# A graph kernel's second pass: gathers tied one by one to TensorE's products, small products placed behind dense ones, and the first block turned in two halves

## The chip, the cores and the metric

The kernel runs on one core of one Trainium2 chip, in one launch. The metric is the device time of that launch in microseconds; less is better. Beside times, a profile of one execution is read: per engine (TensorE = PE, VectorE = DVE, ScalarE = ACT, GpSimd = POOL, SyncE = SP) what ran when, what each waited for, and what the DMA queues moved.

## The reference

Two layers of a graph network over 3327 nodes with 512 features, padded to 3328 = 26 blocks of 128. `adj` is a 3327 x 3327 matrix with few non-zero entries, most of them in the first rows and columns ("hubs"), since the chance of an edge falls with both node numbers.

```python
# layer 0
h = relu(layernorm(x))
g = relu(adj @ (h @ W1) + b1)            # W1: 512 x 128
x = x + adj @ (g @ W2) + b2              # W2: 128 x 512
# layer 1
h = relu(layernorm(x))
attn_a = sigmoid(concat([adj @ h, h]) @ Wa.T + ba)      # one number a node
attn_b = sigmoid(concat([adj @ h, h]) @ Wb.T + bb)
hw = h @ W_sa
scores = (hw @ a_left)[:, None] + (hw @ a_right)[None, :]
e = where(adj != 0, exp(-leaky_relu(scores, 0.01)), 0)
x_a = (e / (e.sum(1) + 1e-5)) @ hw
x_b = adj @ (h @ W_gcnb) + b_gcnb
x = x + sigmoid(attn_a * x_a + attn_b * x_b)
```

## The kernel before, in words

Everything is float32. Columns of `adj` transposed are taken in chunks of 512 (the last of 256); `adj` is used in four ways.

*First pass* (line 549 on): for each chunk, `acc_u` adds 26 dense products of `u = h @ W1` with a 128 x 512 tile of `adj` (L568); the result becomes `g` and is also stored to DRAM. DVE looks through the same tiles (L572), and `make_lists` (L433) makes from that, for every block, lists of the rows with entries: step by step (`yield`), one step for each dense product. POOL gathers by these lists the 128 x 32 pieces of `adj` that have entries (`gather_adj`, `gather_behind`), each tied by `pace` to a dense product.

*Second pass* (L818): `adj @ g`. The last two chunks of nodes (blocks 18 to 25) are "listed": their sums are made from gathered rows of `g` (`gather_g`, 48 gathers) by small products (`list_sums`, L784). The five other chunks (`dense_chunks`, the fifth of 256 columns) are dense: 26 products each (L825), every tile of `adj` loaded by SP. Between the dense products the loop calls generators that record other work:

- `make_h1` (L639): for each block of a finished chunk load `x` (`xb`), add `b2` (L650), the product `px` with `W2` (L663), add it (L666), store, layer-normalise and relu into a row tile (`ln_relu`, L244), two scores (L623), the block's own logits (L630), and store the row to `h_dram` (L637). At a chunk's end the scores of its blocks are transposed by TensorE (`pl`, L687).
- `hubs` (`add_hubs`, L704) and `make_e_hub` (L729): block 0 (the hubs) is dense in layer 1. For every block, `acc_hub[0]` adds a product with `a_hub`, `acc_hub[1]` one with `e_hub`, the exponentials made by DVE and ACT (L709). Row tiles stand in a ring of 12 (`NR`), `e_hub` in a ring of 8 (`EH`).

`SUMS` names the dense products behind which `list_sums` goes a step; the other calls follow from the product's number `n`. `queued(x)` records what follows behind instruction `x` in the order of its engine; beyond that a scheduler decides the order on each engine from the recorded dependencies. After the loop the rest of the hub products is recorded (L871).

*Sparse stage* (L903 on): for blocks 25 down to 1, POOL gathers rows of `h_dram` (194 gathers, which wait until all rows are stored), `attend` (L917) makes their exponentials on DVE and ACT, `sums` (L968) adds small products into `acc` (L981), `turn` (L988) transposes the two sums (`ptt`, L995), `weigh` (L1026) multiplies them with `W_gcnb` (`p_b`, L1035) and `W_sa` (`p_a`, L1042), and `finish` (L875) ends the block and stores it. Adjacency pieces that are not yet gathered follow two a block (`fetch_ae`). The first block to be weighed is block 0, from `acc_hub`: both its halves are turned behind block 25's sums (L1079 to L1082).

Of the kernel before, what the change touches and what calls it, by code (L numbers as in the profile page):

```python
# [50 lines left out]
def kernel(  # L51
# [207 lines left out]
    with (  # L259
# [173 lines left out]
        def make_lists(nth, most):  # L433
# [56 lines left out]
            for batch in batches:  # L490
# [7 lines left out]
                for i, q in batch:  # L498
                    r, k = rooms[i], col[i, q]
                    for h in range(2):  # L500
                        b = NQ * i + 2 * h + q - g0
                        nc.vector.tensor_scalar(
                            at[:, k : k + r, h, :],
                            place_row[:, : r * HALF].rearrange("p (k m) -> p k m", m=HALF),
                            offset[:, b : b + 1], None, op0=ALU.is_ge,
                        )
                    yield
                pl = bank(psB, f"p_list_{f0}")
                plv = pl[:, : m * NT].rearrange("p (c j) -> p c j", j=NT)
# [129 lines left out]
        def make_h1(c, sT, last):  # L639
# [16 lines left out]
            for b, i in enumerate(blocks):  # L656
# [21 lines left out]
                if not extra[i] and i not in LATE:  # L678
                    own_logits(
                        i, made_row(i),  # L680
                        l0w.tile([P, D], BF16, tag="junk", name=f"junk_{i}", bufs=1),
                    )
                yield
            n = w // P
            pl = bank(psB, f"pl_{c0}")
            for b, i in enumerate(blocks):
# [11 lines left out]
            rows_made.update(blocks)  # L698
            yield

        rows_made, unstored = set(), []
        last_row = [None, None, None]

        def add_hubs():  # L704

            def add(k, i, s, n):
                nc.tensor.matmul(  # L709
                    acc_hub[k], s, made_row(i)[:, :D], start=(n == 0), stop=(n == NB - 1)  # L710
                )

            for n, i in enumerate(made_order):
                while i not in rows_made:
                    yield
                add(0, i, a_hub[:, i, :], n)
                if i not in e_hub:
                    make_e_hub()
                yield
                if n:  # L720
                    before_i = made_order[n - 1]
                    add(1, before_i, e_hub[before_i], n - 1)
                    e_added.add(before_i)
                    yield
            add(1, made_order[-1], e_hub[made_order[-1]], NB - 1)
# [25 lines left out]

        g_slots, g_rows, g_taken, g_tile = slots(), {}, [], [None]

        def gather_g(n):
            for f in g_slots:
                k = len(g_taken) % NU
                if not k:
                    g_tile[0] = l0w.tile([P, D], F32, tag="h", name=f"g_row_{f}", bufs=GR // NU)
                t = g_tile[0][:, k * HID : (k + 1) * HID]
                g_taken.append(f)  # L760
                gather(t, g_dram[:, :], row_h[:, f : f + 1], NP - 1)
                g_rows[f] = t
                n -= 1
                if not n:
                    break

        def list_sums():

            for c0, w in listed_chunks:
                acc = bank(psB, f"acc_s_{c0}")  # L770
                for b, i in enumerate(range(c0 // P, (c0 + w) // P)):
                    r = rooms[i] + extra[i]
                    assert fetched[i] == 2 * rooms[i]
                    for k0, k1 in segments(i):
                        for kk in range(k0, k1):
                            for q in range(2):
# [4 lines left out]
                                for h in range(2):  # L781
# [6 lines left out]
                                    )  # L788
                    gather_g(2 * rooms[i])
                    yield  # L790
                s = l0w.tile([P, CW], F32, tag="x", name=f"s_{c0}", bufs=5)
                nc.scalar.copy(s[:, :w], acc[:, :w])
                pt = bank(psB, f"pt_s_{c0}")
                for b in range(w // P):
# [18 lines left out]
        QUIET = 6  # L813
        SUMS = {1: (14, 16, 18, 20, 24), 2: (16, 18, 20, 22, 25)}
        summing = list_sums()
        gather_g(GR)
        order = [i for c0, w in back for i in range(c0 // P, (c0 + w) // P)]
        for c, (c0, w) in enumerate(dense_chunks):  # L818
# [3 lines left out]
            for n, j in enumerate(order):  # L822
# [5 lines left out]
                if c == 0 and n >= 2:  # L828
                    next(lists, None)
                if n in SUMS.get(c, ()):  # L830
                    next(summing)
                elif c and n % 4:
                    gather_behind(added)
                if n % 2 or (c in (2, 3) and n % 4 == 2):
                    with queued(last_e[0] if last and n < 8 else None):
                        next_late()
                if last and n >= NB - QUIET:
                    continue
                if c > 1 and n % 3 == 2:
                    next(hubs)  # L840
                elif c > 1 and (n > 8 if last else n % 3 == 1):
                    with queued(last_row[0] if last else None):
                        make_e_hub()
            if c == 0:
# [11 lines left out]
        while late:  # L856
            next_late()
        for i in unstored:
            store_row(i)
# [11 lines left out]
    with queued(*last_row):  # L871
        for _ in hubs:
            pass

# [28 lines left out]
    with tc.tile_pool(name="spw", bufs=2) as spw:  # L903
# [83 lines left out]

        def turn(i, ty, both_engines):  # L988


            tyT = spw.tile([P, KD, 2, P], F32, tag="tyT", name=f"tyT_{i}")
            for h in range(2):
                pt = bank(psA, f"ptt_{i}_{h}")
# [31 lines left out]

        def weigh(i, tyT, es, cuts=(0, D), sums_first=False):  # L1026

# [5 lines left out]
            for n in (1, 0):  # L1033
                for k in range(KD):
                    nc.tensor.matmul(  # L1035
                        p_b[n][:, :WH], tyT[:, k, 0, :], W_g_sb[:, k, n * WH : (n + 1) * WH],
                        start=(k == 0), stop=(k == KD - 1),
                    )
            p_a = bank(psB, f"p_a_{i}")
            for c0, c1 in zip(cuts, cuts[1:]):  # L1040
                for k in range(KD):
                    last = nc.tensor.matmul(  # L1042
                        p_a[:, c0:c1], tyT[:, k, 1, :], W_sa_sb[:, k, c0:c1],
                        start=(k == 0), stop=(k == KD - 1),
                    )
            return (
# [17 lines left out]

        with queued(last_e[1]):
            for seg in segments(NB - 1):
                made = attend(NB - 1, seg)

        def own_of(i, inst):
# [3 lines left out]

        own_of(LATE[0], made[0])
        fetch_ae(AE_PER)
        for seg in segments(NB - 1):
            added = sums(NB - 1, seg)
        combined.append(added)
        with queued(made[1]):  # L1079
            ty, _ = copy_out(0, acc_hub)  # L1080
        with queued(added):
            tyT, added, copied = turn(0, ty, False)  # L1082
        own_of(LATE[1], copied)
        weighing = 0, tyT, es_hub
        ty, last = copy_out(NB - 1, taken[NB - 1]["acc"])
        turning = NB - 1, ty, taken[NB - 1]["es"]
        held = [copied, last]
        for i in range(NB - 2, 1, -1):
            with queued(*held):
                for seg in segments(i):  # L1090
                    made = attend(i, seg)
            if i == NB - 2:
                own_of(LATE[2], made[0])
            fetch_ae(AE_PER)
# [227 lines left out]
```

## Time and profile before

| | |
|---|---|
| median of 9 runs | 733.88 us (732.98 to 738.29) |
| the profiled execution's own time | 735.72 us |
| its span, first to last instruction | 734.0 us |
| granted TensorE clock, mean | 0.986 |
| dense products of the second pass, `acc_g` (L825) | 112.1 us busy, 260 passes |
| products of the sparse stage, `p_b` (L1035) and `p_a` (L1042) | 97.1 and 93.5 us busy |
| hub products, `acc_hub` (L709) | 104 passes, 281.4 to 413.9 us |
| gathers on POOL: `ae`, `hr`, `rows`, `g_row` | 194, 120, 74 and 48 |
| DMA in the second pass's middle (242 to 322 us) | 320 GB/s, mean busy share 0.96 |

A float32 product appears in the trace as two passes. Their recorded durations overlap, since they are pipelined, so the cost of one is read from start to start: two passes of 512 columns take 0.858 us. A line of the timeline gives the start, the time covered, the engine, the line of the kernel, the operation and, in brackets, how long the engine was idle before and what ended that. By stages of the span: the first pass runs to about 218 us, the second to about 392, the rest of the hub products to 414, and the sparse stage from there to the end.

### The profile page before, as it was taken

The page shows a single profiled execution, that of the slowest core. Times are in us where ns is not written, and L with a number is a line of the kernel's source. Part 1 is how long each engine was busy: PE and PEld are TensorE (multiplying, and loading weights), DVE is VectorE, ACT ScalarE, POOL GpSimd, SP SyncE. Part 2 cuts the span into 40 slices and gives each one's busy share as a digit, 9 for nine tenths or more (in the row PEclk, how much of TensorE's full clock was granted, in tenths as well). Part 3 has the DMA queues.
Part 4 walks back from the last instruction along what each step waited for, and adds up shares of the span by engine and source line. Part 5 has one row for each costly group of instructions (what it writes and reads, how often), then busy time and mean ns, then how long its engine had stood idle before and what let it go on. Part 6 is the DMA issues. An engine that isn't in the chain of part 4 may idle for free.

```text
span 734.0 us, 11907 instructions
## 1 busy us (share of the span) xinstructions
PE 704.7 (96%) x3595; PEld 394.9 (54%) x3595; DVE 507.0 (69%) x1625; ACT 193.8 (26%) x402; POOL 466.8 (64%) x490
## 2 busy tenths in 40 slices
PE   9999988999999999898999899999999999999995
PEld 7775433444464444343455366566565666565653
DVE  7778978999985657988887255556566465746452
ACT  6872000000000124335544112223122222212211
POOL 2400476777765777777666777777777777777400
PEclk9999999999999999999999999999999999999999
DMA  8778899999979999989984856667788888787600
GB/s 274 247 273 265 281 328 289 299 309 290 308 206 309 332 327 360 310 282 321 299 280 136 262 154 201 210 198 219 228 260 275 261 238 275 231 251 235 197 29 33
DMA packets 104889, 185.08 MB, mean 252 GB/s; under 512 B 18401, under 2 KB 35441, under 8 KB 104818
## 3 DMA queue, kind: packets, MB, share of 16 engines
q1 hardware_dynamic: 66544, 113.43, 46.4%
q0 software_dynamic: 23264, 57.64, 27.4%
q10 hardware_dynamic: 15010, 13.18, 5.5%
q8 instruction: 30, 0.49, 0.3%
q14 instruction: 41, 0.34, 0.1%
HBM read 162.29 MB, written 22.26 MB: 251 GB/s over the span
## 4 chain that ended last, share of the span: by engine, by line
PE 75%; DMA 12%; DVE 9%; issue 2%; ACT 1%; POOL 0%; SPq 0%; POOLq 0%; DVEq 0%; ACTq 0%
PE acc_u L568 13%; PE acc L981 13%; PE p_b L1035 13%; PE p_a L1042 12%; PE acc_g L825 8%; DMA a<-in_adjT_dram 6%; DMA xb<-in_x_dram 4%; PE pu L333 3%; PE ptt L995 3%; DVE most L572 2%; PE acc_hub L709 2%; PE pt L325 1%; PE px L663 1%; DVE junk L623 1%; DMA x<-xb 1%
## 5 line engine op out<-in xcount | busy, mean ns | idle before, releaser
L166 POOL DMA_INDIRECT ae<-in_adjT_dram,row_a x194 | 203.4, 1049 | 126.4 <-DVE past L519 54.3
L568 PE MATMUL acc_u<-a,rows 128*128 128x512 f32 (+1 forms) x364 | 160.6, 578 | 5.2 <-DMA a<-in_adjT_dram 5.2
L166 POOL DMA_INDIRECT hr<-h_rows,row_h x120 | 122.6, 1022 | 36.9 <-issue 22.9
L572 DVE TENSOR_REDUCE most<-a 128x16 f32<-128x512 f32 (+1 forms) x182 | 112.0, 639 | 12.8 <-DMA a<-in_adjT_dram 12.5
L825 PE MATMUL acc_g<-a,g 128*128 128x512 f32 (+1 forms) x260 | 112.1, 565 | 0.7 <-DMA a<-in_adjT_dram 0.7
L568 PEld LDWEIGHTS acc_u<-a,rows 128*128 128x128 f32 x364 | 66.1, 194 | 63.9 <-issue 48.8
L1035 PE MATMUL p_b<-W_g_sb,tyT 128*128 128x257 f32 x416 | 97.1, 385 | 0.8 <-ACT tyT L1008 0.5
L166 POOL DMA_INDIRECT rows<-h_rows,row_h x74 | 77.7, 1050 | 25.3 <-issue 11.9
L1042 PE MATMUL p_a<-W_sa_sb,tyT 128*128 128x512 f32 (+2 forms) x216 | 93.5, 576 | 0.0
L1035 PEld LDWEIGHTS p_b<-W_g_sb,tyT 128*128 128x128 f32 x416 | 76.5, 189 | 30.9 <-DVE ae L249 5.7
L1010 DVE COPY tyT<-ptt 128x512 f32<-128x512 f32 x51 | 34.9, 687 | 71.1 <-PE ptt L995 71.1
L825 PEld LDWEIGHTS acc_g<-a,g 128*128 128x128 f32 x260 | 48.6, 194 | 49.9 <-issue 41.8
L166 POOL DMA_INDIRECT g_row<-g_rows,row_h x48 | 51.5, 1072 | 19.5 <-issue 13.7
L1042 PEld LDWEIGHTS p_a<-W_sa_sb,tyT 128*128 128x128 f32 x216 | 40.9, 189 | 37.8 <-issue 35.9
L981 PE MATMUL acc<-hr,ae 64*64 64x512 f32 x480 | 57.7, 598 | 0.0
L884 ACT ACTIVATE f<-f 128x2 f32<-128x2 f32 x26 | 5.3, 203 | 164.2 <-DVE f L883 141.1
L343 ACT ACTIVATE gT<-acc_u,b_col 128x512 f32<-128x512 f32 (+1 forms) x7 | 4.6, 657 | 150.5 <-DMA a<-in_adjT_dram 93.7
L623 DVE SCALAR_TENSOR_TENSOR junk<-rows,w_rows 128x512 bf16<-128x512 f32 x52 | 35.7, 687 | 4.6 <-ACT rows L244 3.6
L981 PE MATMUL acc<-rows,ae 64*64 64x512 f32 x296 | 36.3, 609 | 1.9 <-DVE ae L251 1.9
L981 PEld LDWEIGHTS acc<-hr,ae 64*64 64x64 f32 x480 | 26.0, 135 | 20.0 <-issue 19.7
L995 PEld LDWEIGHTS ptt<-ident,ty 128*128 128x128 f32 x208 | 24.2, 141 | 14.7 <-issue 13.9
L666 DVE TENSOR_TENSOR xb<-px,xb 128x512 f32<-128x512 f32 x26 | 17.2, 683 | 21.4 <-PE px L663 21.4
(159 smaller groups left out, 938.1 us busy)
## 6 DMA issues: line engine op xcount, KB each, us to landing
a<-in_adjT_dram SPq DMA_DIRECT2D x286, 256.0 KB
h_rows<-rows SPq DMA_DIRECT2D x26, 260.0 KB
x<-in_x_dram SPq DMA_DIRECT2D x26, 256.0 KB
xb<-in_x_dram SPq DMA_DIRECT2D x26, 256.0 KB
x<-xb ACTq DMA_DIRECT2D x26, 256.0 KB
x1b<-x SPq DMA_DIRECT2D x26, 256.0 KB
out_dram<-va SPq DMA_DIRECT2D x25, 256.0 KB
ae<-in_adjT_dram,row_a POOLq DMA_INDIRECT x194
```

What stands on the lines that cost most here:

```text
L166: return nc.gpsimd.indirect_dma_start(out=dst, out_offset=None, in_=table, in_offset=bass.IndirectOffsetOnAxis(ap=rows, axis=0), bounds_ch ...
L333: nc.tensor.matmul(pu[:, :HID], hT[:, k, :], W1_sb[:, k, :], start=(k == 0), stop=(k == KD - 1))
L568: added = nc.tensor.matmul(acc[:, :w], u[j], a[:, :w], start=(j == 0), stop=(j == NB - 1))
L572: nc.vector.tensor_reduce(most[:, : w // GW, j], a[:, :w].rearrange("p (b i) -> p b i", i=GW), axis=AX.X, op=ALU.max, apply_absolute_value ...
L623: return nc.vector.scalar_tensor_tensor(junk, h, 1.0, w_rows[:, s, :], op0=ALU.mult, op1=ALU.mult, accum_out=into)
L666: nc.vector.tensor_tensor(x1, px, x1, ALU.add)
L825: added = nc.tensor.matmul(acc[:, :w], g[j], a[:, n % per, :], start=(n == 0), stop=(n == NB - 1))
L981: added = nc.tensor.matmul(taken[i]["acc"][h][q * HALF : (q + 1) * HALF, :], both[half_p, q * n + k, :], taken[i][k0][k][half_p, q, :D], s ...
L995: moved = nc.tensor.transpose(pt[:, k * P : (k + 1) * P], ty[h][:, k * P : (k + 1) * P], ident)
L1010: last = nc.vector.tensor_copy(dst, src)
L1035: nc.tensor.matmul(p_b[n][:, :WH], tyT[:, k, 0, :], W_g_sb[:, k, n * WH : (n + 1) * WH], start=(k == 0), stop=(k == KD - 1),)
L1042: last = nc.tensor.matmul(p_a[:, c0:c1], tyT[:, k, 1, :], W_sa_sb[:, k, c0:c1], start=(k == 0), stop=(k == KD - 1),)
```

## The change

1. In `make_lists` a step is added between the making of a batch's flags (`at`) and its products.
2. The transposes of a chunk's scores leave `make_h1` for a function `turn_logits`; it is called behind the second block of the next chunk's `make_h1` (for the last chunk at once).
3. `gather_g` fetches one row set, and `gather_one` is called from the loop for one gather at a time: of `g` while slots are free, else of `adj`. Each is tied by `pace` to the dense product it stands behind and recorded behind the gather before it. A running sum `owed` (0.93 for a dense product, more where px or hub products stand) sets how often: one each 1.4. Before, 24 gathers of `g` were issued at once and the others after each block's list sums, and `gather_behind` stood behind three products of four.
4. All that the loop records behind a dense product (list sums, px, hub products, exponentials) is placed behind that product in TensorE's order (`queued(added)`). px begins at the third product of a chunk. `SUMS` is changed, and the copy and transposes of the list sums are two steps.
5. The rest of the hub products is recorded by `rest_of_hubs`: first pairs, then all of `acc_hub[0]`, then `acc_hub[1]` but for three, then block 0's first half is turned, then the last three.
6. Block 0's `p_b` comes ahead of block 25's sums, its second half is turned there, and blocks 25 and 24 are summed and block 25 turned before block 0's `p_a`.

```diff
@@ make_lists
                     yield
+                yield
                 pl = bank(psB, f"p_list_{f0}")
@@ make_h1
+                if b == 1 and unturned:
+                    unturned.pop()()
                 yield
+            unturned.append(lambda: turn_logits(c0, w))
+            if last:
+                unturned.pop()()
+            yield
+
+        def turn_logits(c0, w):
             n = w // P
+            blocks = range(c0 // P, (c0 + w) // P)
...
+        added_hubs = [0, 0]
+        def add_hub(k, i, s, n):
+            added_hubs[k] += 1
+            return nc.tensor.matmul(
+                acc_hub[k], s, made_row(i)[:, :D], start=(n == 0), stop=(n == NB - 1)
+            )
+        def rest_of_hubs(k, until):
+            last = None
+            for n in range(added_hubs[k], until):
+                i = made_order[n]
+                while k and i not in e_hub:
+                    make_e_hub()
+                with queued(last):
+                    last = add_hub(k, i, e_hub[i] if k else a_hub[:, i, :], n)
+                if k:
+                    e_added.add(i)
+            return last
...
+        def gather_g():
+            n = len(g_taken)
+            f = g_slots[n]
+            if n % NU == 0:
+                g_tile[0] = l0w.tile([P, D], F32, tag="h", name=f"g_row_{f}", bufs=GR // NU)
+            g_rows[f] = g_tile[0][:, n % NU * HID : (n % NU + 1) * HID]
+            g_taken.append(f)
+            return gather(g_rows[f], g_dram[:, :], row_h[:, f : f + 1], NP - 1)
+        def gather_one(matmul):
+            n = len(g_taken)
+            with queued(last_g[0]):
+                if n < len(g_slots) and n // NU * NU < len(g_summed) // NU * NU + GR:
+                    made = gather_g()
+                else:
+                    made = next(columns, None)
+            if made is not None:
+                pace(made, matmul)
+                last_g[0] = made
@@ list_sums
-                    gather_g(2 * rooms[i])
+                    g_summed.extend(2 * rooms[i] * [i])
                     yield
                 s = l0w.tile([P, CW], F32, tag="x", name=f"s_{c0}", bufs=5)
                 nc.scalar.copy(s[:, :w], acc[:, :w])
+                yield
@@ the loop
-        SUMS = {1: (14, 16, 18, 20, 24), 2: (16, 18, 20, 22, 25)}
+        STEP, SPACE, owed = 0.93, 1.4, 0.0
+        SUMS = {1: (14, 16, 18, 20, 21, 25), 2: (17, 20, 22, 25), 3: (0, 4)}
-        gather_g(GR)
...
-                if n in SUMS.get(c, ()):
-                    next(summing)
-                elif c and n % 4:
-                    gather_behind(added)
-                if n % 2 or (c in (2, 3) and n % 4 == 2):
-                    with queued(last_e[0] if last and n < 8 else None):
-                        next_late()
...
+                with queued(added):
+                    if n in SUMS.get(c, ()):
+                        next(summing)
+                    owed += STEP * w / CW
+                    if late and n % 2:
+                        owed += STEP / 2
+                    if c > 1 and n % 3 == 2:
+                        owed += STEP
+                    if (c or n > 2) and owed >= SPACE:
+                        owed -= SPACE
+                        gather_one(added)
+                    if n > 2 and (n % 2 or (c in (2, 3) and n % 4 == 2)):
+                        with queued(last_e[0] if last and n < 8 else None):
+                            next_late()
...
     with queued(*last_row):
-        for _ in hubs:
-            pass
+        for _ in range(EH):
+            make_e_hub()
+        for n in range(*sorted((added_hubs[1], NR + 6))):
+            rest_of_hubs(0, n + 1)
+            rest_of_hubs(1, n + 1)
+        added = rest_of_hubs(0, NB)
@@ weigh
             p_a = bank(psB, f"p_a_{i}")
+            with queued(between(last) if between else None):
...
@@ sparse stage
+        nc.scalar.copy(ty[0], acc_hub[0])
+        with queued(added):
+            added = rest_of_hubs(1, NB - 3)
+        with queued(added):
+            tyT, added, copied = turn(0, ty, False, halves=(0,))
+        with queued(added):
+            added = rest_of_hubs(1, NB)
+        hub_e_copied = nc.scalar.copy(ty[1], acc_hub[1])
...
+        def first_sums(added):
...
+            with queued(added):
+                _, added, copied = turn(0, ty, False, tyT, (1,))
+            for i in (NB - 1, NB - 2):
...
+                for seg in segments(i):
+                    with queued(added):
+                        added = sums(i, seg)
...
+            b, ty_b, es_b = turning.pop(0)
+            with queued(added):
+                tyT_b, added, copied = turn(b, ty_b, False)
...
+        with queued(added):
+            added, add_es, end = weigh(0, tyT, es_hub, between=first_sums)
```

## The prediction

> **What bounds the kernel now.** I read the page's busy shares and chain first, then the second pass in stretches of 8 us, then each engine's instructions in order of time where TensorE (PE) has a hole, and last the instruction order of the two built programs, engine by engine.
>
> ```profile
> PE 704.7 (96%) x3595; PEld 394.9 (54%) x3595; DVE 507.0 (69%) x1625; ACT 193.8 (26%) x402; POOL 466.8 (64%) x490
> PE 75%; DMA 12%; DVE 9%; issue 2%; ACT 1%; POOL 0%; SPq 0%; POOLq 0%; DVEq 0%; ACTq 0%
> ```
>
> PE is busy 96% of the span, so an edit that leaves its work as it is can win only the holes. The chain leaves PE for 25% of the span, and the stretches (PE busy, PEld, DVE, ACT, POOL, granted clock, DMA share, GB/s) show where:
>
> ```profile
> 242.00:250.00 8.00, 8.00 (x19) 3.34 (x19) 4.75 (x15) 1.89 (x5) 6.03 (x7) 1.00 1.02 334
> ...
> 258.00:266.00 8.00, 7.66 (x61) 3.26 (x60) 3.32 (x10) 1.11 (x2) 6.17 (x7) 1.00 1.05 376
> ...
> 290.00:298.00 8.00, 4.93 (x14) 1.94 (x13) 6.92 (x22) 0.39 (x2) 6.33 (x6) 0.97 1.02 365
> 298.00:306.00 8.00, 8.00 (x18) 3.10 (x18) 6.68 (x27) 4.02 (x6) 6.30 (x6) 0.82 0.91 287
> ...
> 346.00:354.00 8.00, 6.30 (x13) 3.10 (x14) 7.48 (x24) 2.85 (x7) 6.17 (x7) 0.79 0.96 329
> ```
>
> PE's holes lie where VectorE (DVE) is at 85 to 94%, and the DMA engines are full there. A hole also costs after its end: the granted clock is 0.82 and 0.79 in the stretch behind or around it.
>
> ```profile
> 297.05 0.32 PE L687 MATMUL pl<-ident,node 128*128 128x128 f32 x1 [2.54 <-DVE junk L623]
> 347.70 1.13 PE L663 MATMUL px<-W_sb,sT 128*128 128x512 f32 x2 [3.37 <-DVE xb L666]
> ```
>
> Both come from px products issued four in a row: DVE needs some 4.7 us a block behind each (five 128x512 operations at 0.61, seven for half of the blocks, four of 128x128 at 0.20, small ones), and PE stands at a transpose of scores (L687) or at the next px. The last kind of hole is the hand-over to the sparse stage (the last number is POOL's idle time, then PE's):
>
> ```profile
> 390.91 1.88 PE L663 MATMUL px<-W_sb,sT 128*128 128x512 f32 x4
> 401.39 0.99 POOL L166 DMA_INDIRECT rows<-h_rows,row_h  x1 [3.01 <-DVE e_hub L251]
> 416.40 3.15 PE L981 MATMUL acc<-rows,ae 64*64 64x512 f32 x16 [1.93 <-DVE ae L251]
> 430.36 2.81 PE L981 MATMUL acc<-hr,ae 64*64 64x512 f32 x24
> ```
>
> The last rows leave PE at 392.6; the first gather of rows starts at 401.4 (8.8 later), block 25's sums at 416.4 (15.0 behind the gather). DVE's mask for block 24 ends at 426.1 (24.7 behind the gather), 4.3 before PE asks for it. From 401.4 to 689.4 POOL issues 216 gathers, 1.333 us each, with one gap over 0.45: the sparse stage begins when the first gather does.
>
> **The change, part by part.** *PE's work does not change*: one dense product of 512 columns costs 0.858 us start to start, one of 256 columns 0.43, a hub or px product 0.858, a transpose 0.109; the 200 passes of list sums with their edges took 8.1. From the second chunk's first dense product (242.7) to the end of px 17, before: 78 x 0.858 + 26 x 0.43 + 26 x 0.858 + 27 hubs x 0.858 + 8.1 + 32 x 0.109 = 135.2 us. Measured: 392.6 - 242.7 = 149.9. So 14.7 us are lost there; the holes above, two waits on loads (0.5 each at 254 and 258) and one of 1.4 at 367 make 12 of them.
>
> *Small products behind dense ones* spreads px to one every 3.5 to 7 us of PE time up to px 14; a px that is held back holds back its block's addition, stores and scores. In the new order PE reaches the end of px 12 after 124.0 us of work and px 17 after 135.6 (28 hub products before it). If nothing else stalled, nearly all 14.7 would be won. But the fifth chunk has 256 columns, and the new order puts eight px (20, 21, 12 to 17) into it where the old one had six. Behind px 12's addition DVE's queue holds, up to px 17's addition, 26 wide operations x 0.61 + 24 hub-score operations (128x128) x 0.20 + 15 small x 0.08 = 21.9 us, while PE needs 11.6 to px 17. With the addition after px 12 (0.65) and one wait for ScalarE, DVE adds px 17 at 124.0 + 22.9 = 146.9, eleven us behind PE. Before, DVE idled 2.7 us until px 16. From that addition to the first gather it took 7.4 us (393.97 to 401.39); 0.4 more for a second bn_stats now in between. First gather: 154.7, before 158.7: only 4.0 earlier.
>
> *The first block's halves turned apart* puts p_b of block 0 (16 x 0.216 = 3.5) and two transpose groups (0.44 each) ahead of block 25's sums, which covers that wait; p_a of block 0 (3.43) and block 25's transposes (0.87) now stand behind block 24's sums. POOL, not PE, times those: six gathers, two of adjacency and six more at 1.30, so block 24's mask still ends 24.7 behind the first gather. Then 24 products 2.74, plus 1.7 for a cold clock (the same 24 took 4.5 at 416.4 and 2.74 at 430.4), 0.87 + 3.43 + 0.2: block 25's p_b starts 33.6 behind the first gather; before, 433.1 - 401.4 = 31.7. So 1.9 us are given back, and PE waits about 5 us twice. What these waits hide: the loads of W_g, which still follow the last row's store.
>
> *Gathers paced one by one.* In the second pass POOL already starts one each 1.30 us; the new spacing, 1.4 / 0.93 dense products of 0.858, is 1.29. So the wait costs PE nothing and seldom binds; behind a waiting gather stand only later gathers, and the list sums that wait for those have up to 24 rows fetched ahead. But the new order leaves ten more adjacency gathers to the sparse stage: 10 x 1.333 = 13.3 us on a POOL that is never idle there. What covers them: between a block's last gather and its first product lie 10.1 us at block 24, 10.8 at 21, 23.8 at 9, 22.2 at the second half of 2, and 6.5 are needed (block 25's). The extra ones stand behind blocks 14 to 10; left are 23.8 - 13.3 = 10.5 and 22.2 - 13.3 = 8.9, plus the 1.9 by which PE comes later. Cost zero; without the cover, up to 4.
>
> *What stays lost in the second pass.* The second and third chunk move 80 us x 320 GB/s = 25.6 MB at a DMA share of 0.96. Their work in the new order is 69.5 us, which asks for 368 GB/s. From the rows: at 376 (best 8 us) nothing is lost; at 320 / 0.96 = 333 the bytes need 76.9, 7.4 lost. I take 355, the mean of the stretches with a share over 1: 72.1, so 2.6 lost, say 3, and 1 for small waits; both ends stay, 0 to 8.
>
> The Trainium skill, "DMA: Bandwidth & Descriptors" (section "Where 436 GB/s comes from"), gives a core about 358 GB/s of HBM, which speaks against the change: by it 71.5 us, 2.0 lost. The same page (section "Measured") has 425 for a core whose neighbour is idle, by which nothing is lost; 376 is the most that an 8 us stretch here shows.
>
> The Trainium skill, "TensorE: Matmul & The Clock Gate" ("Why this matters for your kernels"), lets the clock fall only after gaps of about 3 us; by it the cold 1.7 would follow only the 5 us waits. Here it fell to 0.82 behind a hole of 2.5.
>
> *The added step of the lists* moves their products one dense product later; the 1.45 us wait at 202.4 (its cold clock makes it 3.7) is for a batch that stays where it was. From 3.7 won to 1 lost; I take 0.3 won.
>
> **Sum.** 154.7 - 158.7 + 1.9 + 4.0 - 0.3 = +1.6. Against the profiled span of 734.0 that is 735.6; the median is 733.88, so 735.5. The profiled run's own time was 735.72, 1.7 above its span.
>
> **The rivals.** (a) *Faster, the spreading pays in full.* If DVE followed px 17 as before (first gather 8.8 behind it), the gather would start at 135.6 + 4 + 8.8 = 148.4 instead of 158.7, and with 1.9 given back the end comes 8.4 earlier: 725.5. For it: all holes of 290 to 367 come from bursts that the new order ends, and DVE is only 78% busy over the stretch. Against: the 22 us queue behind px 12, which idle time earlier cannot shorten. It decides if the first gather comes under 10 us behind px 17.
> (b) *Slower, loads become the bound in the second and third chunk.* At 333 GB/s 7.4 are lost instead of 3, and PE's clock drops after waits for loads; 1.7 for one such fall: 735.5 + 4.4 + 1.7 = 741.6. For it: a share of 0.96 over 80 us, and two load waits at 254 and 258 already. Against: PE ran at full clock through 242 to 250 beside 334 GB/s. It decides when those chunks hold under 345 GB/s.
> (c) *The pacing does nothing*, since POOL's own 1.30 is as long as the spacing. Likely, and part of the forecast; it has no time of its own.
>
> **How the numbers follow.** Forecast (spreading wins, the hand-over takes it back): 0.44, own range 731 to 739. (a) 0.31, around 725. (b) 0.25, around 742. Nothing below 0.3% (2.2 us) can be told from no change. Faster: 0.30 of (a) and 0.06 of the forecast, 0.36. Within: 0.01 of (a) and 0.24 of the forecast, 0.25. Slower: (b) and 0.14 of the forecast, 0.39. The range for 8 in 10: 723 to 743.
>
> **What would show it.** Right: px products at least 3 us apart and no PE hole over 2 us between 280 and 370; a first gather 17 to 22 us behind px 17, near 397 to 402; two PE waits of 3 to 6 us before the sums of blocks 25 and 24; 226 gathers from the first row gather on. Wrong: a first gather before 393 (rival a), DMA waits of several us on the dense products (rival b), or PE waiting on gathers from block 9 on, which would mean that the ten extra gathers are not covered.

## The result: 745.3 us, slower by 1.6%

| | before | after |
|---|---|---|
| median, runs in turn on one chip | 734.27 us (31 runs) | 745.34 us (10 runs) |
| ratio, 95% interval | | 1.0164 (1.0140 to 1.0189) |
| span of the profiled execution | 734.0 us | 747.3 us |
| first dense product of the second chunk | 242.7 us | 242.5 us |
| first gather of rows | 401.4 us | 413.2 us |
| from the first gather to the end | 332.6 us | 334.1 us |

Of the 13.3 us between the spans, 11.8 lie before the first gather of rows, all of them behind the start of the second chunk. The page's busy shares and chain of the changed kernel:

```profile
PE 707.2 (95%) x3595; PEld 394.7 (53%) x3595; DVE 507.5 (68%) x1625; ACT 197.2 (26%) x404; POOL 464.1 (62%) x490
PE 39%; DMA 2%; DVE 2%; issue 1%; ACT 0%; POOL 0%; DVEq 0%; POOLq 0%
```

PE has the same 3595 instructions. The chain's shares sum to 44%, 329 us: it was followed back through the sparse stage alone, whose length hardly changed, and says nothing of what came before. The stretches of 8 us that were shown of before (PE busy, PEld, DVE, ACT, POOL, granted clock, DMA share, GB/s):

```profile
242.00:250.00 8.00, 8.00 (x20) 3.62 (x19) 1.29 (x2) 0.58 (x1) 6.03 (x7) 1.00 1.03 350
258.00:266.00 8.00, 8.00 (x85) 4.00 (x85) 6.58 (x20) 1.11 (x2) 6.22 (x6) 1.00 1.03 361
290.00:298.00 8.00, 6.71 (x17) 2.78 (x16) 6.10 (x20) 4.63 (x6) 6.48 (x6) 1.00 0.97 318
298.00:306.00 8.00, 8.00 (x59) 3.42 (x61) 7.94 (x32) 5.83 (x11) 5.44 (x6) 1.00 1.04 348
346.00:354.00 8.00, 8.00 (x20) 3.53 (x19) 6.61 (x21) 1.40 (x3) 5.11 (x6) 1.00 0.79 245
```

In these stretches the holes of before are smaller or gone: PE's 4.93 us became 6.71, its 6.30 became 8.00, and the clock is full. So the local effect of the placing is there. The timeline shows where the time went instead:

```profile
324.23 0.66 PE L835 MATMUL pt_s<-ident,s 128*128 128x128 f32 x4 [2.15 <-ACT s L831]
...
385.63 0.48 PE L698 MATMUL pl<-ident,node 128*128 128x128 f32 x1 [4.00 <-DVE junk L624]
386.75 3.42 PE L664 MATMUL px<-W_sb,sT 128*128 128x512 f32 x4
...
392.59 1.88 PE L664 MATMUL px<-W_sb,sT 128*128 128x512 f32 x4
413.24 1.16 POOL L166 DMA_INDIRECT rows<-h_rows,row_h  x1 [21.30 <-DVE e_hub L256]
429.11 3.69 PE L1034 MATMUL acc<-rows,ae 64*64 64x512 f32 x16 [5.55 <-DVE ae L251]
436.47 4.30 PE L1034 MATMUL acc<-hr,ae 64*64 64x512 f32 x24 [2.04 <-DVE ae L251]
```

In the fifth chunk PE stands for 4.0 us at transposes of scores that DVE has not made. The last px leave PE at 394.5, but the first gather starts 18.8 us later; before, it was 8.6 (392.8 to 401.4). POOL had stood idle for 21.3 us: it waits for the last rows. Then block 25's and block 24's sums wait for their masks, 5.6 and 2.0 us.

DVE's own instructions: the additions of b2 (L651) and of px (L667), each with the idle time ahead of it.

```profile
359.27 0.69 DVE L651 TENSOR_TENSOR xb<-xb,b_row 128x512 f32<-128x512 f32 x1 [1.65 <-DMA xb<-in_x_dram]
...
368.17 0.69 DVE L651 TENSOR_TENSOR xb<-xb,b_row 128x512 f32<-128x512 f32 x1 [2.49 <-DMA xb<-in_x_dram]
...
380.74 0.69 DVE L667 TENSOR_TENSOR xb<-px,xb 128x512 f32<-128x512 f32 x1
...
403.95 1.29 DVE L667 TENSOR_TENSOR xb<-px,xb 128x512 f32<-128x512 f32 x2
```

The line at 380.74 adds px 12, which had left PE at 375.6: DVE is 5.2 us behind already there. The line at 403.95 adds px 16 and 17. DVE's busy time over three stretches (columns as above), first the changed kernel, with the sum:

```profile
280.00:320.00 40.00, 38.70 (x189) 17.29 (x188) 34.55 (x122) 19.04 (x33) 27.39 (x26) 1.00 0.94 314
320.00:360.00 40.00, 37.85 (x91) 16.80 (x90) 26.94 (x85) 16.04 (x26) 24.06 (x23) 0.96 0.86 271
360.00:395.00 35.00, 30.23 (x98) 18.40 (x97) 27.89 (x96) 16.22 (x28) 23.69 (x23) 0.90 0.71 223
sum 115.00, PE 106.78 PEld 52.48 DVE 89.38 ACT 51.30 POOL 75.15; mean PE 35.59 PEld 17.49 DVE 29.79 ACT 17.10 POOL 25.05
```

The kernel before, the sum of the same three:

```profile
sum 115.00, PE 107.32 PEld 52.88 DVE 95.30 ACT 53.00 POOL 85.33; mean PE 35.77 PEld 17.63 DVE 31.77 ACT 17.67 POOL 28.44
```

Up to 395 DVE has done 89.4 us of work where it had done 95.3: it idles from 320 to 360 and has the last eight blocks left. PE's sums, 106.8 and 107.3, say that over the whole stretch its holes moved and did not shrink. Two reasons are possible. Either px come too late in PE's order (B). Or rows of x come too late (A); SP's queue speaks for that. Its waits from 320 to 395 (total, times, longest), of the changed kernel:

```profile
SPq L649 <- DMA x<-xb: 18.3, 5, 5.8
```

SP stood 18.3 us at loads of x (L649) until a tile of the ring was stored; before, its loads of x (L648) show no such wait. A third theory (C) was that the new order of the hub products delays the last rows.

### The profile page after: what moved, and what is told of

Read it like the earlier page. It is cut to its first block, busy times and chain, and to the rows that moved or that the text cites. A ratio compares the mean times of both kernels' runs of the same rounds, so it can differ in the third digit from the quotient of the medians.

```text
span 747.3 us, 11922 instructions
## 1 busy us (share of the span) xinstructions
PE 707.2 (95%) x3595; PEld 394.7 (53%) x3595; DVE 507.5 (68%) x1625; ACT 197.2 (26%) x404; POOL 464.1 (62%) x490
## 5 line engine op out<-in xcount | busy, mean ns | idle before, releaser
L166 POOL DMA_INDIRECT ae<-in_adjT_dram,row_a x194 | 200.3, 1033 | 135.7 <-DVE most L573 55.2
L166 POOL DMA_INDIRECT hr<-h_rows,row_h x120 | 124.0, 1033 | 36.8 <-issue 23.7
L166 POOL DMA_INDIRECT rows<-h_rows,row_h x74 | 76.7, 1036 | 43.6 <-DVE e_hub L256 21.3
L1034 PE MATMUL acc<-hr,ae 64*64 64x512 f32 x480 | 59.4, 614 | 2.0 <-DVE ae L251 2.0
L1048 PEld LDWEIGHTS ptt<-ident,ty 128*128 128x128 f32 x208 | 24.3, 142 | 16.2 <-issue 13.7
L651 DVE TENSOR_TENSOR xb<-xb,b_row 128x512 f32<-128x512 f32 x26 | 17.7, 688 | 20.9 <-DMA xb<-in_x_dram 18.0
```

The lines of the kernel that those rows point to most:

```text
L166: return nc.gpsimd.indirect_dma_start(out=dst, out_offset=None, in_=table, in_offset=bass.IndirectOffsetOnAxis(ap=rows, axis=0), bounds_ch ...
L651: nc.vector.tensor_tensor(xs[i], xs[i], b2_row, ALU.add)
L1034: added = nc.tensor.matmul(taken[i]["acc"][h][q * HALF : (q + 1) * HALF, :], both[half_p, q * n + k, :], taken[i][k0][k][half_p, q, :D], s ...
L1048: moved = nc.tensor.transpose(pt[:, k * P : (k + 1) * P], ty[h][:, k * P : (k + 1) * P], ident)
```

## The experiments

The first four kernels ran on a chip on which the kernel before took 829.3 us; there only comparisons among them are used, and each ran again where it takes 734 (e6, e13, e7, e8). Two notes on the expectations: with the list sums in their old places (e10, e12, e18) blocks 18 to 21 come ahead of 8 to 11 and not behind them, so px 20 stands elsewhere than in the changed kernel, and the distances named for it are not to be relied on; and they count 120.8 us of work up to px 12 in the changed kernel where the forecast had 124.0. Times of single products and gathers are from one profiled execution each, which can lie some us from its kernel's median (e6's by 3.7, e15's by 7). Counting from the second chunk's start leaves out the first pass, whose length differs by some 5 us between executions.

**px early in a chunk again (e1, e6).**

```diff
-                    if n > 2 and (n % 2 or (c in (2, 3) and n % 4 == 2)):
+                    if n % 2 or (c in (2, 3) and n % 4 == 2):
```

> The changed kernel (745.3 us), except that px steps may stand behind the first three products of a chunk again. That gives back six steps: px 12 ends after about 114.8 us of PE's work in the second pass instead of 120.8 (counted from the products in the built order), px 20 after 101 instead of 106. Theory A (loads: DVE idled 18.0 us for rows of x, because a load waits for one of five tiles whose store is late, and stands in SP's queue): the steps come earlier but the loads do not, so the waits of DVE for x stay at 15 to 20 us and the time at 743 to 747. Theory B (steps: the px steps were simply handed out too late, and the last eight pile up on DVE): the first gather comes about 5 us earlier, 408 instead of 413.2, and the time is 739 to 741. Theory C (hand-over): no change, 745.

> As e1 (px steps also behind the first three products of a chunk), against the changed kernel of the same call. Theory A (loads): 0 to 2 us below it. Theory B (steps): first gather about 5 us earlier, 4 to 6 us below it. Theory C (hand-over): no difference.

Measured: e1 807.4 us, 0.973 (0.968 to 0.978) of the kernel before there. e6 733.2 us, 0.9986 (0.9960 to 1.0011); the changed kernel measured beside it (e5, below) took 743.7. The edit wins 10.5 us, about twice what theory B gave, while DVE's waits for x stay at 15.3 us (18.6 in e5). The first gather is at 402.4, 6.5 earlier; counted from the second chunk's start it comes at 160.2 instead of 169.2. The rule `n > 2` lets px begin at a chunk's fourth product, not at its third; it drops one px step in the second and fifth chunk and two in the third and fourth. A block has two steps, so six steps are three blocks.

**Six tiles for x (e2, e13).**

```diff
-                    xs[i] = l0w.tile([P, D], F32, tag="x", name=f"xb_{i}", bufs=5)
+                    xs[i] = l0w.tile([P, D], F32, tag="x", name=f"xb_{i}", bufs=6)
...
-        tc.tile_pool(name="adjp", bufs=8) as adjp,
+        tc.tile_pool(name="adjp", bufs=7) as adjp,
```

> The changed kernel with six tiles instead of five in the ring that holds rows of x, and seven instead of eight tiles of adjacency, which pays for it. Theory A (loads): DVE's waits for rows of x fall from 18.0 us to under 10 and SP's waits at these loads from 28 us to under 12; the first gather comes 4 to 8 us earlier and the time is 737 to 741. Theory B (steps): DVE waits less in the middle but the last px still leave PE at the same place, so the first gather moves by under 2 us and the time stays at 743 to 746. One tile of adjacency less could cost up to 3 us by waits for loads in the first pass, which the trace would show there.

> The changed kernel with six tiles in the ring of x and seven of adjacency, as e2, on a chip of the usual kind. Theory A (loads are the cause): DVE's waits for x under 10 us (18.0 in the changed kernel), the first gather 4 us earlier or more, 737 to 741. Theory B (the px steps are handed out late, and the waits for x only fill time in which DVE has nothing else): the first gather moves by under 2 us, 742 to 746, whatever becomes of the waits for x.

Measured: e2 813.6 us; its first gather came 175.6 us behind the second chunk's start, as e3's did (176.0), where e1 and e4 have 164.3 and 166.6. e13 748.0 us, 1.0201 (1.0160 to 1.0242). DVE's waits for x fall from 18.6 us in e5 to 13.7, not under 10:

```profile
  DMA xb<-in_x_dram: 13.7, 8
```

Counted from the second chunk's start (239.7 in e5, 245.2 in e13) the first gather comes at 166.9 instead of 169.2. So the ring could account for some 2 us, little more than the 1.6 between two executions of the changed kernel itself (170.8 and 169.2). The second chunk starts 5.5 later than in e5 and 2.7 later than in the latest kernel with eight tiles of adjacency, which is what the missing tile costs. Theory A has the smaller part; that the other waits for x follow from the lateness (a tile is free when its block is stored) was argued, not shown.

**The old hand-over (e3, e7).** Parts 5 and 6 undone, all else as changed.

```diff
-        for _ in range(EH):
-            make_e_hub()
-        for n in range(*sorted((added_hubs[1], NR + 6))):
...
+        for _ in hubs:
+            pass
```

> The changed kernel with the hand-over of before: the hub products pair by pair, block 0 turned as a whole behind block 25's sums, p_b and p_a together (parts 5 and 6 undone). From the first gather to the end the changed kernel took 334.1 us, the one before 332.6. Theories A and B (all is lost before the first gather): the first gather stays at 412 to 414 and 1 to 2 us are won, 743.5 to 744.5. Theory C (the new hand-over makes the last rows late, since the products of acc_hub and the exponentials stand in another order): the first gather comes at 404 or earlier and the time falls to 735 to 738.

> As e3 (parts 5 and 6 undone), against the changed kernel of the same call. Theories A and B: 1 to 2 us below it, first gather where it was. Theory C: first gather 8 us or more earlier and 7 to 10 us below it.

Measured: e3 819.8 us, 0.984 (0.975 to 0.993); e7 746.7 us, 1.0175 (1.0135 to 1.0215). The first gather is where it was (407.5; 408.9 in e5), so theory C falls. From it to the end e7 takes 335.4 us against 333.1, since PE waits longer ahead of block 25's sums:

```profile
423.33 3.69 PE L1030 MATMUL acc<-rows,ae 64*64 64x512 f32 x16 [6.82 <-DVE ae L251]
```

In e5 that wait is 5.54. The medians, 743.7 and 746.7, have intervals that overlap: the new hand-over may be worth up to 3 us here, and no cost of it shows.

**The old placing (e4, e8, e16).** Part 4 undone, but for the copy and transposes of the list sums, which stay two steps.

```diff
-        SUMS = {1: (14, 16, 18, 20, 21, 25), 2: (17, 20, 22, 25), 3: (0, 4)}
+        SUMS = {1: (14, 16, 18, 20, 22, 24), 2: (16, 18, 20, 22, 24, 25)}
...
-                with queued(added):
+                with queued(None):
...
-                    if n > 2 and (n % 2 or (c in (2, 3) and n % 4 == 2)):
+                    if n % 2 or (c in (2, 3) and n % 4 == 2):
```

> The changed kernel with part 4 undone: px, hub products and list sums are no longer held behind a dense product, px steps come from the second product of a chunk on, and the list sums stand where they stood. Pacing, the scores' transposes and the hand-over stay new. px comes in bursts of four again, with PE's holes of 2 to 4 us beside them, but px 12 after 108.8 us of PE's work. All of theories A and B put the loss into part 4, so the first gather should be back at 400 to 403 and the time at 734 to 737. Theory C (hand-over) or a cost of the pacing leaves it at 742 or more.

> As e4 (part 4 undone), against the changed kernel of the same call. Theories A and B: first gather about 11 us earlier, 8 to 11 us below it, so level with the kernel before within 2 us. Theory C: no more than 3 us below it.

> e8 once more (part 4 undone), to see whether it beats the kernel before: 0.985 to 0.9935 of it in e8's four runs. Expected again 0.986 to 0.994.

Measured: e4 802.4 us, 0.964 (0.957 to 0.971); e8 727.4, 0.9893 (0.9851 to 0.9935); e16 729.5, 0.9942 (0.9918 to 0.9966). Part 4 costs all of the loss and more, 14 to 16 us, and what is left of the change beats the kernel before. e5 stands beside e6 to e8:

> The changed kernel itself beside the kernel before, since the chip of the first four runs took 829 us for the kernel before, where 734 was measured at first. If this is a chip like the first one: 734 for the kernel before, 745 for this one, ratio 1.014 to 1.019, first gather near 413. If it is a slow one: 829 for the kernel before; the changed kernel with all its parts should lie beside the runs e1 to e4 there, 800 to 830, and its distance to them is what their edits are worth on that chip.

Measured: 743.7 us, 1.0146 (1.0097 to 1.0196).

**Which piece of part 4 (e12, e14).** e12 is e6 with the list sums where they were, e14 is e6 without the holding:

```diff
# e12, against e6
-        SUMS = {1: (14, 16, 18, 20, 21, 25), 2: (17, 20, 22, 25), 3: (0, 4)}
+        SUMS = {1: (14, 16, 18, 20, 22, 24), 2: (16, 18, 20, 22, 24, 25)}
# e14, against e6
-                with queued(added):
+                with queued(None):
```

> e6 (held behind dense products, px also behind the first three) with the old places of the list sums besides; against e8 it differs only in that the small products are held behind their dense product. px 20 stands at 89.5 us of PE's work (79 in e8), px 12 at 110.5 (108). Theory B (lateness of px is the whole loss): half way between e6 (733.2) and e8 (727.4), 728 to 731. If the holding itself costs beyond the lateness: level with e6, 732 to 734, and e8's gain over it comes from bursts that DVE can work through while PE goes on.

> e6 (px steps from the start of a chunk, 733.2) without the holding behind dense products, but with the new places of the list sums. If holding costs what is left between e6 and e8: 726 to 730, level with e8. If it is the places of the list sums together with the holding that cost: 731 to 734.

Measured: e12 732.9 us, 0.9996 (0.9977 to 1.0016); e14 733.9, 1.0025 (0.9994 to 1.0055). Each alone wins nothing over e6's 733.2; both together (e8, e16) win 4 to 6. Neither is therefore a price of its own. Lateness of px 12 alone does not explain it: px 12 ends 126.7 us behind the second chunk's start in e6, 124.3 in e14 and 120.3 in e12, but 122.0 and 122.5 in e8 and e16, the faster ones.

The traces show a second difference. Ahead of block 12 DVE goes through the same eight blocks in every kernel (8 to 11 and 18 to 21). From its addition of the first of these px to that of px 12 it works 33 to 39 us everywhere, but beside that it waits 16.5 us in the changed kernel, 15 to 16 in e5, e7 and e13, 14.7 in e6, 7.6 in e14, 4.7 in e12, 5.9 in the kernel before and 2 to 3 in e8, e10, e11 and e15 to e18. The waits are for rows of x and for ScalarE, which takes the root and makes the row within a block. In e6 (321.8 to 371.5), then in e8 (322.6 to 362.7):

```profile
DVE xb L651 <- DMA xb<-in_x_dram: 7.3, 3, 3.7
DVE ln_b L239 <- ACT ln_b L238: 3.1, 5, 1.1
DVE junk L624 <- ACT rows L244: 2.5, 3, 0.9
DVE e_hub L251 <- ACT e_hub L250: 1.3, 1, 1.3
```

```profile
DVE e_hub L251 <- ACT e_hub L250: 1.2, 1, 1.2
DVE ln_b L239 <- ACT ln_b L238: 1.2, 2, 0.9
```

So with part 4 DVE does not work more, it waits more. No run changes these waits alone, and the medians of e12 and e14 do not follow them; why each piece alone wins nothing stays open.

**The rest, part by part (e9, e10, e11, e18).** e9 is the kernel before with parts 5 and 6, e10 with parts 1, 2, 5 and 6, e18 with part 2 alone; e11 is e8 with more gathers in the second pass:

```diff
# e11, against e8
-        STEP, SPACE, owed = 0.93, 1.4, 0.0
+        STEP, SPACE, owed = 0.93, 1.25, 0.0
# e18, against the kernel before
+                if b == 1 and unturned:
+                    unturned.pop()()
                 yield
+            unturned.append(lambda: turn_logits(c0, w))
+            if last:
+                unturned.pop()()
+            yield
+
+        def turn_logits(c0, w):
...
```

> The kernel before with parts 5 and 6 alone (new hand-over). The forecast gave 1.9 us back for them: then 735 to 737, about 2 us above the kernel before of this call. Against it stands e7, where undoing them made the changed kernel 3 us slower: then 2 to 4 us are won here too, 730 to 732, and the wait of PE ahead of block 25's sums (1.9 us and a cold clock in the kernel before) is covered by p_b of block 0.

> The kernel before with parts 1, 2, 5 and 6: neither the paced gathers (3) nor the new placing (4). e8, which has part 3 besides, took 727.4 where the kernel before took 734.0. If the pacing costs nothing and wins nothing, as the forecast had it, this is level with e8 within 2 us: 726 to 730. If the pacing is what won the 6.6 us of e8, it stays near 732 to 734. In the built order parts 1 and 2 alone bring px 20 from 88 to 79 us of PE's work, since the transposes of scores no longer stand ahead of the next px; if that is what wins, this run is at least 3 us below e9.

> e8 with SPACE 1.25 instead of 1.4, so that 22 adjacency gathers are left to the sparse stage, as in the kernel before, instead of 32. The forecast priced the ten at 0, up to 4 without their cover. If they are covered: 727 to 728, level with e8 within 1 us. If they set the sparse stage: from the first gather to the end 2 to 4 us less than in e8 (335.7), so 723 to 726.

> The kernel before with part 2 alone (the transposes of a chunk's scores behind the second block of the next chunk). In the built order px 20 comes at 79 us of PE's work instead of 88, as in e10. If part 2 is what wins in e10 and e16: 728 to 731, 0.992 to 0.996 of the kernel before. If it needs the new hand-over to become time: 732 to 734.5.

Measured: e9 732.9 us, 1.0011 (0.9985 to 1.0037), no change that can be told: the 2 to 4 us won are out, the 1.9 given back (1.0026) lies inside the interval. e10 728.8, 0.9936 (0.9903 to 0.9969), level with e16: no gain or cost of the pacing shows. e11 733.0, 0.9984 (0.9959 to 1.0009): 22 gathers left over instead of 32 win nothing; against e8 and e16 they lose 3 to 6 us. POOL in e11:

```profile
395.24 1.00 POOL L166 DMA_INDIRECT ae<-in_adjT_dram,row_a  x1 [0.30 <-issue]
396.55 1.00 POOL L166 DMA_INDIRECT ae<-in_adjT_dram,row_a  x1 [0.30 <-PE acc_hub L719]
397.85 1.00 POOL L166 DMA_INDIRECT rows<-h_rows,row_h  x1 [0.30 <-issue]
```

px 17 is added at 382.9 there, 2.2 us earlier than in e8, but the adjacency gathers ahead of it in POOL's queue hold the first gather of rows to 397.9, 4.7 later than in e8.

e18 has the lowest median, 726.0 us, 0.9908 (0.9876 to 0.9940), but its interval overlaps with those of e8, e10 and e16. So part 2 alone gives as much as any of these kernels shows. Its three stretches:

```profile
280.00:320.00 40.00, 38.13 (x191) 17.30 (x190) 38.53 (x140) 19.49 (x37) 31.92 (x27) 1.00 0.95 320
320.00:360.00 40.00, 40.00 (x102) 18.19 (x101) 37.81 (x127) 19.61 (x33) 31.61 (x28) 1.00 1.03 363
360.00:395.00 35.00, 34.99 (x113) 20.14 (x113) 27.60 (x96) 18.77 (x36) 27.38 (x26) 1.00 0.65 200
```

PE is without a hole from 320 on and DVE does 103.9 us of work up to 395 instead of 95.3. The transposes that stood 2.54 us at 297 in the kernel before now come behind the next chunk's first px, when the scores are long made; and from 345 us on the px come in pairs in place of bursts of four (345.7, 358.0, 366.8 and 380.1 in the trace; one burst of four is left at 327.2). px 17 leaves PE 139.7 us behind the second chunk's start (150.1 before). What is left is POOL's queue, as in e11: eight adjacency gathers start behind px 17's addition at 382.4, and the first gather of rows starts at 394.7, 12.3 later (8.1 in the kernel before).

**Two waits that are left (e15, e17).** e15 is e8 with two adjacency gathers moved behind block 24's rows; e17 is e8 with the third chunk's first hub product left out at n = 2:

```diff
# e15
-            fetch_ae(AE_PER)
...
-                    fetch_ae(AE_PER)
+                    fetch_ae(2 * AE_PER)
# e17
-                    if c > 1 and n % 3 == 2:
+                    if c > 1 and n % 3 == 2 and (c > 2 or n > 2):
```

> e8, with the two adjacency gathers between the rows of blocks 25 and 24 put behind the rows of block 24. In e8 PE waits 3.7 us at 413 for block 24's mask and runs 4 us more at a lower clock. The two gathers are 2.6 us of POOL, so the mask comes 2.6 earlier: the wait falls to about 1.1, the cold clock behind it should go, and 2.5 to 4 us are won against e16. If another wait stands right behind (the masks of block 23, 2.6 us later), nothing is won.

> e16 with the first hub product of the third chunk left out at its third dense product, so that hub products begin three dense products later. In e16 PE waits 3.62 us at 289.3 for DVE's e_hub. If PE's holes in the second pass count in full: the wait goes and up to 3 us are won, 0.989 to 0.992 of the kernel before. If DVE's work to the last row sets the first gather: level with e16, 0.992 to 0.997, since DVE has the same list to go through.

Measured: e15 728.6 us, 0.9926 (0.9899 to 0.9953), level with e16; the wait for block 24's mask, 3.71 us in e8 and 2.23 in e16, is 1.85. In this execution, the longest of its eight, PE waits 4.3 us for ScalarE's copy of a later block's sums (0.9 in e8, 2.4 in e16). e17 729.4, 0.9963 (0.9934 to 0.9993), also level, but it doesn't decide: the wait didn't go, it moved from 289 to 292 and still took 3.18 us.

## Why the prediction was wrong

**The step that failed: when DVE adds px 12.** The forecast let PE end px 12 after 124.0 us of work plus 4.0 lost, and had DVE free at that moment ("With the addition after px 12 (0.65) and one wait for ScalarE, DVE adds px 17 at 124.0 + 22.9 = 146.9"): with the 4.0, px 12 would be added at 128.0. Measured from the second chunk's start, px 12 ends at 133.1, 9.1 lost instead of 4.0 (5.1 more; PE's holes up to there are 5.2, 1.8 of them for loads, and the clock's fall at 325, 0.57 over 4 us, is some 1.7), and is added at 138.3, since DVE still stands at blocks 18 to 21: of the 5.2 us between it works 3.1 and waits 2.1 for ScalarE. So the end of px 17's addition comes 29.7 us behind px 12 instead of 22.9 (6.8 more). From there to the first gather 8.0 pass instead of 7.8. Together 12.1: the first gather comes 170.8 behind the chunk's start, 158.7 were forecast. In the second execution of the changed kernel (e5) px 12 ends at 131.0, is added at 137.0, and the first gather comes at 169.2.

The forecast counted DVE's queue behind px 12, 21.9 us, and that was nearly right: between the two additions lie 23.8, of which DVE works 22.2. In all sixteen profiled executions on chips where the kernel before takes 734 us these two additions lie 21.1 to 24.7 apart, so the addition of px 12 sets the first gather, where POOL's queue does not. What the forecast did not count is what stands ahead of px 12, although it had seen that px 20 and 21 had moved into the fifth chunk. The bound of "8 lost" came from loads; no case priced px that come late. e6 shows the price: six px steps, 10 us.

Two small readings were off and change little: the last px leave PE at 392.8, not 392.6, and the two waits for loads near 254 and 258 took 0.34 each, not 0.5.

**Spreading px.** Right as a mechanism for the holes (290 to 298, 346 to 354), wrong as a gain: a held product delays its block's whole chain on DVE, and DVE's list to the last row sets the first gather. Nor was the sign of no hole over 2 us between 280 and 370 met: PE stands 2.15 us ahead of the list sums' transposes at 324. No run that holds px beat the kernel before; e8 and e18 do not hold them.

**The hand-over, +1.9.** The stretch behind the first gather is 1.5 us longer, with two waits of PE, 5.6 us and 2.0 where about 5 was foretold for each. But two executions of one kernel differ about as much there (334.1 and 333.1 for the changed one, 335.6 and 334.0 for e8 and e16), so neither the 1.9 nor its absence is shown. Without parts 5 and 6 (e7) the stretch is longer, 335.4.

**Ten more adjacency gathers at no cost, pacing at no cost.** No cost of either shows: 226 gathers stand from the first row gather on, as foretold, and behind the wait at 436 PE is never idle for 0.8 us or more; e10 is level with e16. It wasn't seen that gathers left in the second pass delay the first gather of rows once the rows are early.

**Loads, 3.0.** Dense products waited 1.8 us for them (1.44 at 275 and 0.33 at 278). Rival (b) is out by these waits and by PE, which was busy for 34.2 of 36 and 38.7 of 40 us (244 to 280 and 280 to 320). Its own sign, under 345 GB/s, would have let it in: the two stretches moved 335 and 314. That sign was badly chosen, since a rate under the limit can also mean that less was asked for. **The lists' step, -0.3:** the second chunk starts 0.2 earlier, less than executions of one kernel differ there (242.5 and 239.7), so nothing is shown.

**Rival (a), 725.5,** is about what e18 reaches, by the part that the forecast gave no value: it had the hole of 2.54 us at L687 in its hands and put its end down to the spreading, not to the moved transposes. That the numbers agree is partly luck: in e18 the first gather comes at 152.5, not at 148.4 as in (a), and the stretch behind it takes 331.7 instead of 334.5.

## What to carry to other kernels

Behind an engine that must finish a list before the next stage starts, ask first how early its inputs are handed over, and only then how evenly: here six steps of delay cost 10 us, while the holes that the spreading mended (3.5 us in the two stretches shown) came back elsewhere and did not show in the time. A queue is to be counted from where it is last empty, not from the instruction at which one starts looking. The wait that closes a batch (here transposes of the last scores) belongs behind the first products of the next batch.

## What the runs showed of the hardware

A hole of 2.15 us on PE cost clock in one run and none in another. Granted clock (the number before the last two) in the 4 us behind the same wait at the transposes of list sums, first in the changed kernel, then in e7:

```profile
325.00:329.00 4.00, 4.00 (x7) 1.54 (x5) 2.44 (x7) 2.57 (x7) 1.00 (x1) 0.57 1.04 366
```

```profile
320.00:324.00 4.00, 4.00 (x10) 1.71 (x9) 1.95 (x6) 2.62 (x7) 2.20 (x2) 1.00 1.04 355
```

The Trainium skill, "TensorE: Matmul & The Clock Gate" ("What's actually happening"), has the gate look at a window of about 3.4 us that runs free of the kernel; that agrees with one hole having two outcomes, though by the page a whole window must be idle and 2.15 us are less.

The same kernel before took 734 us on one chip and 829 on another. In e1 to e4, which ran there, PE was busy for 90 to 91% of the span instead of 95 to 96. Every stage was longer, the sparse one most: 381 to 384 us from the first gather to the end, where the other chips took 332 to 339. What slowed that chip is not shown. Kernels with px early or free were ahead of those with px late there too (802 and 807 against 814 and 820).
